# A transformer block on one core: query and key weights prepared in pairs, the values' first halves cast by VectorE, a new written order

## The chip, the cores and the metric

The kernel runs on one core of one Trainium2 chip. The metric is the device time of one execution in microseconds (us), median of several runs. Engine names as in the profile: PE is TensorE's matrix multiply, PEld its weight load, DVE is VectorE, ACT is ScalarE, POOL is GpSimd, SP is the engine whose queue issues the transfers.

## The reference

The input x has 8 sequences of 512 rows of 512 numbers. The block is attention, then a feed-forward part, each behind a layer norm and added to its input:

```
x = x + layernorm(attention(layernorm(x)))
x = x + layernorm(ffn(layernorm(x)))

attention: qkv = x @ w_attn + b_attn; 16 heads of 32; q and k are rotated by an angle
           that depends on head and column; causal softmax(q k^T) * 512**-0.5; times v; @ w_proj + b_proj
ffn:       y = quantised(layernorm(x)) @ ternary(w_fc).T ; gelu ;
           quantised(layernorm(.)) @ ternary(w_proj).T
ternary(w) = sign(round(w / (mean|w| + eps))) * mean|w|
```

All is float32. The kernel works with 16-bit matrix products and keeps the precision by splitting a number in two halves: `hi` is the number rounded to 16 bits, `lo` is what is left, rounded too.

## The kernel before, in words

**Work.** Attention goes by sequence b (8) and by group g of four heads (4 in a sequence); the feed-forward part goes by 128 rows (32 pieces). Each of these is a generator that records instructions and yields between steps. Every generator family has a letter: N normalises 128 rows of x, Q makes a group's queries and keys (12 + 12 matmuls of 512 columns, line 570), V makes 128 rows of values for 8 heads (12 matmuls of 256 columns, line 540), S makes a group's scores and their masked maxima (matmul 604, maxima on VectorE 618, 16 of them a group), A the exponentials and their halves (ScalarE 651 and 657, GpSimd 659, and a transposing transfer, 518), W the weighted sum of the values (686), G, P the projection, X, Z and C the feed-forward part (matmuls 817 and 873).

**Order.** The program order is written out as one string, `ORDER` (4345 letters): each letter takes the next step of that family, and `pin()` ties each instruction to the one before it on its engine. So every engine, and SP's queue of transfers too, does its instructions in the order in which the string recorded them. An instruction that waits holds all behind it on its engine. Tiles come from pools with a fixed number of buffers: PSUM has three `sc` tiles of two banks and two `mm` tiles of one bank.

**Start-up.** Before the first sequence can flow, weights are prepared (H, J, B, R, T, Y), which takes roughly the first 80 us, mixed with work of the first sequences:

- H and J call `make_qk_weights(s, g)` (227): s is 0 for queries and 1 for keys. The 128x512 block of the weight is transposed by a product with a unit matrix (235), copied to SBUF (240) and its rows' squares are summed (241); from the sums and the bias VectorE makes a bound per row and spreads it on a diagonal (244 to 247); one product with a matrix of ones brings all rows' bounds to every partition (254), VectorE takes the maximum (257), and from it makes a power of two as the scale (258 to 261). The transposed block is turned by the rotation angle (253), and is cut in two 16-bit halves (264 ScalarE, 266 VectorE). Then follow the scale of the scores and that of the bias (267 to 276). This is done 8 times. `rot`, an `sc` tile, is held from line 253 until line 266 has read it.
- R is `make_proj_weights`: row means of the projection's weight (350) are taken off (357, GpSimd), the largest magnitude is taken (367), its power of two gives the scale (373 to 379), and two halves are cut (383 to 386).
- `values` (V) ends in two reads of the same PSUM tile: ScalarE casts the first half (553), VectorE makes the second as a difference (555). The tile `mm` is free after both.

Of the kernel before, what the change touches and what calls it, by code (L numbers as in the profile page):

```python
# [10 lines left out]
F32 = mybir.dt.float32  # L11
F16 = mybir.dt.float16
BF16 = mybir.dt.bfloat16
I32 = mybir.dt.int32
# [21 lines left out]
nNwHwHHNNnwJHJwJNNNtNTNBNnHJBBBBBBBBNRNNHNJHRNRRBBNHNNHHHwJJRtTJJJHHNNBNnwHwBNJNRJJHwHRRNNNJHJJJ  # L36
RRttttttBHnwTNTNNJTNNNNNNQQHHTTTYJQQYYYHHNHHYtYHQYtYJQQQQIQHHJBYJYQQQHJTQQQSYYSQYQYSAQQttYYQQBtV
VSHSAQQAJAVYYNStVSAAAASYQQQAAAAAAJASQQQQAAQAAABBQQQVJQSASVVVSAAVnARVJVVAAJnVVVVnVSASAAAVVVARAVAV
VVSTTASQQQAVQQSQVVWWWVWnWAATWQVQVQQNNNAWWATWWSWNSWAWNNANNVAAAAAANWWVNVNVASNAAnQAANSAAAASWQSSTSAN
NASrAWNNWWAAGWAGASWWWWWWNAAWGVAAAAVAVAAVSVNNQSAAQQQWVVSQSVAAAAVAAQSAQVSGGGQQSAVAWSQWWWVWAAQQRRSA  # L40
AWWWWWWWAAAAAAQVWARVARAWQQQSSRAARQAAtSAAtQQQQQSSGAGAASQAWArWVWGWWAAWWVWWQWWWWWVASQQTTAGGSSYVGQAA
SAQAQAYAYYYYQSQYQQQYSPPAQPAYPPYAQAPSAWPSPAWVVVVFVAVVFAAAAAWAWWAPWYWPFFPPnPASSQQPWSVQFWnWAQAFWWAA
WSVSAQVAAFYQAAAAWAYQQSASVQQPNNSYPASQNFAAYAAAXQXXNNFAAANNXXNFXAXXPFXSPXFPGFPSrNWNVNWVNPSWWWAAWVGP
NSWAZAWWWWWAWAVAAVVAAVFSSVANVNYNAVAAYAYPVZSYVXZPPXXWZAAAAPXXXPGXPPXAFAGZFSXSrQWGQWnWZZXAWQWQVWSW
QWAZZQQWWQSSAAAZQWSQQWQZZCAAAAFZWWAAAAPCZAAAQSQSAAZCGQSCQQAAAAZSGQGCCWCZSVAAAWPGCVSVCCSVAASWWCWA
AAQAQWWCCQWQWSWWVWAAZQWAQNFVVFQVASWSQAAAVVQZAVFVSAWQGQGQQWAQASQZZCVQGVWWSPAAAWXWXXSAAQWnnQSQXAAA
VVQPSWWQFFNZWZPQPWPAAAWWAANZZZZrSZANAQAFXrQVPQVFXAWPQAXSVVQCQNXNCANPSPXCZWAnNWNNCASWWWNNWCQAAAFF
XSQPGZZCPGCAASWPWNSWPAnNFFSWCNZNAPVAAWWAASWXZVXXNPZNZNNPCCAAZFAZCVVVWAAAACAXASAVVVVZSZSZQSAVVXQX
QXFXFWPFVQXQQPAAWPXQPQFFSWNWNPAFFSWCCQAWPCZXAQZCXFPZCXrZZFAAAAAZQPFQFFPPCXZPZCZPGGGWWWWWWWAAASXC
PCFWSXCXPVXFSVAXAWAAZZASZCAAAZZZCCZCQAAVWVGCQZXAZZCCQZCSSCQCWWSCSWGAAQQWQCQSXZCGAGAQCWWXFXQPWWFA  # L50
AAAWWZZrAAAASCAWCACAAFCVQAAQCCWXXVXVVVGPNASGGZVZVSAAQXVQVZSQVPAFFQVXQSAFVQnPSXPNWWQAPQPnQWQWWFSA
AAAAZZZZPCZXWACZSCWWWWWCWZQQAVWAACZVAASXFSPPrWSXZXZZCSXAAVASSAVACQPGAAAACFASQASAAZCAACFXFXQXQXWZ
CCQGCXQQPXZFWrQWQWPWWPCZZZXPQFAFZXZZZPFNWCWZNXAACXWAQCWAAACWCNZAWCWZAPPNZZQCFXNNNPPSFFFFSFZnPCCN
ZNZAAXNnSCCPCZXXPZXXANNNNZXVPCACCrWNVZCZXCVVVZCVZASAANSAPSZCXASZCVAVAAAVCZAAZSSAAVVCVSQZPCCASAAA
AXCQCWWSQVCPQVXXWQQWXQWVFVNWQCrPAZQPZZZQPGGGXAPGFZZAQWSQXAQPSCWWAWQWWWACQASNXFACFZZFQCAAASWFCZWW
CAAZAQFQQCGGSXCFQWPWZZZXWWPSAAAAAGAQNFACXACAQAZWSFFFXCSACVWWVnWWWZAAQSQPFXXZZWVXXWAAGVVNXFXSQZAG
FXAQVVSQAGSSZQXXZQCCZVVQZAAAAZQFVQAXSQVVAWFCFFQAZCWZACQAQPCPZXSCSCWPCWPCASXWrAZWZAZZPZZXXZAAAAFA
CWCAAVAACCXCVSnAZSQPPVVrSPPSQCPWWWWWPQPAXAAAQSZZPCAZQFQZZFWCAAZZZSPPQCQCAAAWQFCQCQWCWNNCXWWXWSWG
PAAAAnXQVNGCAFCFFCWWWWWWWNCNNNWAAZVVFXVZAANZZCCNSVAPVSPAVSSVSFrNNAAAAFPAAACPSAAAAANXCNPAXFACXZZn
CXCXSSXZZNVNZFNCASXAPPCVVZACCAVFFCACCAAXXZZSXSXPFQCCPQrNWWFWAQWPXQXXWXPGGWSZZGQFZZQZZCWWZNXPAAAA  # L60
GWPWSAANAAZCZPWWWCAQSCQCQAZAZCQCZSQFAWGQAAZZACQSZQWCCCCQAAWSQQQVXZVSVVQWNWQWPAWQAPVGGQCWAVWWWWWW
XXAnAWSAQQASZSVVXZFGPFXXSQXQGZGCXQFAPAFFAASQASFPZZAAAAQQSAPAFAQAAPZXXQACSAQCSQQQZFFnCSCVWCWVAAZZ
APSWWWWVCFVVrWAWWVCPAZAZZWWAVVVWWAAASFAWnCZZACVCVVSXAAASPZCQFZZZCCXQACAASXAAAQXQQQQSQCSXQWCXCXQN
NXCXCANWCWWCWWZZFSNNNAAACANNAFAAXNNQNNNZQnFFZCVCGCGXWWWXWZWAWWWAFXCCVNFVVVSPNNVPXArZSSSZZAZAVPVS
QNAAAACSAAAAAPZAXXPQXXAQXPPZPPrQQPSQXSPAZQNPPZPZXSQXQFCQXCSAAPXCZZZZSWWCWCWWCAAAAAAFFAZAQAAZQVZC
AVXAZCVVPZAXPXWXPCZCSCFFFXPGGGWWZWPCXWCSWQWFQWFPCAGCAZAQSZSZAWACQZZAQQZCSSFAAACAAAZQNZWPGQCAFrQC
QCSWFQZQZACAVWVVGWWWCVWWWWWVWWCGACAZVAACSWGFVSSVFZVGXVXXVVVGSQXPAAAQPSAAZAVASXXQACrSVVPAQAFQPXFS
AFZAAQAZPXPFQWXZPZQZZNXCPSPPPAAQPQPWnWSWPZnWWQQCPZVCAAWZAAAASAFFFVVnZAVZSCZSCQCQWWQWQCWAWCAASAAA
SAAQQQAAWQCQXQZZNNZXNZCANZZWSXCCNAAACQNCNNCCXASSCWCQVCAZXNNNSCNSNWCWWXCWWCXXAFFAAZAAAGGWWWAWWFNA
rWNNWSCXAAAXVXWSCCCQXQQFVXZAAZAAQAVSVSSXAZPPFQQFAQSFZZZVAFAAAVXVQXPQXQXPZQQWWPXPZCSCArVPPZXZZZZV  # L70
XWWWVVVCVCXAZAXCWPPAZZAPVAVPXCPFZCPFZZZGFGGWSSCPWWWAZCSAAGAZAXPSQSWCQWWZAZZFAQFFFFXCQAXXAAACCWAF
AAACAASCZQCCXXQAZCXZQZACZSrCZQZCQASSWGWCAAWCWWZWACZGXWSCXSQXAAPPZCZCWWWWWWAAAACVAZCSrXZFGAXVQWQX
VXSXAZQCVCSFFFSQAGXPCQCAQCFSFCAZQZQZGZGASQCZAAAAAQCQAWSQQQCXZZFAZZZZAVCXCVVVXWPWAPWAAAAAFPAFWCCP
XPFPXWXVXCPWPFPFXZFZFSXASZCZrZZPVXZPZXPXXAVVACSXAPCSCQZZZZSACWWWWWQCAWAZACAQZFCSPFZPFFFPAFFAXXQW
CCQXQXAZZCCAZZCACWXXCrCZZZPACSWCSZPCPWCSPSCWWCAZZAZPAQAWSQXAZAZFASAAGGWAPPAAFQFXSAPQXCAFFSWWWZXZ
AZAQQPWAPSWWCFCCWPGAAAZAAAAXXPXXSXGAZGPAXAZCFSZZZAPCZSZZVVAFVVAAPAAZZAZACSCCSCGCCCCFAZArWSXZWWWW
WWWWWWWWXWXFSFAFASCASGAACCAPAFFAAAAAAZXAZXXCFXXXXZZZXXXXFCZFFFXZZZCCCGXCXWWCCXCWWWWWWWWWWWWZZGGC
GGZrZZZCXXCCXXZZCPXPZPCPCZPCZPPPCCZZrZFFXXCFFZZZZFXCFZFXCPCCZPCXCXCZZCCPXXZZCPPZPZCPZPFFFXFXPrXP
ZCPCCPPFPPZFZFZPXZZZCFZFXCXXCXXZZZFZCFPCXCCFFPFZCZXXXXZXCPXCCrXPPZZXPPPZZZZXFZZFXCZZFFZZFFFZCXCC
XCXCXXCZZZZCXXCCCCZCCZCZCXZXZZCCXCXXCXXCZZZZZZZZXZCXXCCZZCXZZXCZZZCZZCCCCCCCCCCZZCCCZZZZZCCZCCCC  # L80
CCCCCCCCCCCCCCCCCCCCCCCCC
# [4 lines left out]
def block_kernel(  # L86
# [40 lines left out]
    def sc_tile():  # L127
        return ps_sc.tile([P, 2, 512], F32, tag="sc", name="sc")
# [31 lines left out]
    def power_below(dst, src):  # L160

        nc.vector.tensor_scalar(
            dst.bitcast(I32), src.bitcast(I32), 0x7F800000, None, ALU.bitwise_and
        )

# [50 lines left out]
    qk_top = const.tile([P, 2 * NG], F32)  # L216
# [10 lines left out]
    def make_qk_weights(s, g):  # L227
        w = wraws.pop((s, g))

        n = s * NG + g
        pst = sc_tile()[:, 0, :]
        for k in range(NE):
            nc.tensor.matmul(pst[:, ts(k, P)], w[:, k, :], turns[:, NG, :], start=True, stop=True)
        yield
        wT = x1p.tile([P, E], F32, tag="x1", name="wT")
        sq = tp.tile([P, E], BF16, tag="q", name="sq", bufs=2)
        longest = tiny(2, f"long{s}")
        nc.scalar.copy(wT, pst)  # L240
        nc.scalar.activation(sq, pst, AF.Square, accum_out=longest[:, 0:1])
        yield
        b2 = longest[:, 1:2]
        nc.vector.tensor_tensor(b2, bqk[:, n : n + 1], bqk[:, n : n + 1], ALU.mult)
        nc.vector.tensor_scalar(b2, longest[:, 0:1], 2.0 * E, b2, ALU.mult, ALU.add)
        diag = tp.tile([P, P], BF16, tag="qT4", name="diag", bufs=2)
        nc.vector.tensor_scalar(diag, ident_h, b2, None, ALU.mult)
        yield

        ps = sc_tile()  # L250
        rot = ps[:, 0, :]
        for k in range(NE):
            nc.tensor.matmul(rot[:, ts(k, P)], wT[:, ts(k, P)], turns[:, g, :], start=True, stop=True)
        nc.tensor.matmul(ps[:, 1, 0:P], ones_b, diag, start=True, stop=True)
        yield
        top, sc = tiny(name=f"wtop{s}"), tiny(name=f"wsc{s}")
        nc.vector.tensor_reduce(top, ps[:, 1, 0:P], AX.X, ALU.max)
        nc.vector.tensor_scalar(top, top, 4.04, 2.0**-60, ALU.mult, ALU.max)
        root_power(top, top)
        nc.vector.reciprocal(sc, top)  # L260
        nc.vector.tensor_scalar(sc, sc, 2.0 ** (12 - 65) / X_S, None, ALU.mult)
        yield
        hi, lo = (wqk[s, g][:, h, :] for h in range(2))
        nc.scalar.activation(hi, rot, AF.Copy, scale=sc)
        yield
        nc.vector.scalar_tensor_tensor(lo, rot, sc, hi, ALU.mult, ALU.subtract)
        nc.vector.tensor_scalar(qk_top[:, n : n + 1], top, 2.0 ** (65 - 12), None, ALU.mult)
        nc.vector.tensor_scalar(
            bqk[:, n : n + 1], bqk[:, n : n + 1], sc, X_S, ALU.mult, ALU.mult
        )  # L270
        if s:
            nc.vector.tensor_tensor(
                e_scale[:, g : g + 1], qk_top[:, g : g + 1], qk_top[:, n : n + 1], ALU.mult
            )
            nc.vector.tensor_scalar(
                e_scale[:, g : g + 1], e_scale[:, g : g + 1], -1.0, None, ALU.mult
            )
        yield
# [756 lines left out]
```

## Time and profile before

| | |
|---|---|
| median of 3 runs | 1046.0 us (1045.74 to 1046.53) |
| profiled execution | 1048.4 us, its span 1046.6 us |
| PE busy | 974.4 us, 93% |
| ACT busy | 906.1 us, 87% |
| DVE busy | 824.9 us, 79% |
| POOL busy | 757.5 us, 72% |
| instructions | 22733 |

How to read it: an engine's busy time is the union of its instructions' spans. A group row gives line, engine, operation, the tile written and those read, shapes, then total busy time and the mean duration of one in ns, and behind the bar the engine's idle time just before these instructions and what ended it. A window row gives, for a stretch of time, busy us of each engine (instructions in brackets), the granted clock of TensorE as a fraction, and the transfers. The means of instructions that stand directly behind each other on an engine overlap a little at their ends: 512 maxima with a mean of 545 ns would be 279 us, but are busy for 253.4 us.

### The profile page before, as it was taken

What the parts mean: (1) busy time and instruction counts of PE and PEld (TensorE: products, weight loads), DVE (VectorE), ACT (ScalarE), POOL (GpSimd) and SP (SyncE); (2) the same over time, 40 slices, a digit from 0 to 9 for tenths busy, and PEclk for the clock granted to TensorE, in tenths of its full rate; (3) what the DMA queues carried; (4) which work ended last, traced back from release to release, by engine and by line L of the source; (5) the groups of instructions that cost most, each with busy time, mean ns of one, the idle gap of its engine ahead of it and who ended that gap; (6) DMA issues with size and microseconds to landing.
All of it is one profiled execution on the core that took longest, in us unless ns stands there. A gap on an engine that the chain in (4) does not pass through costs nothing.

```text
span 1046.6 us, 22733 instructions
## 1 busy us (share of the span) xinstructions
PE 974.4 (93%) x8258; PEld 509.0 (49%) x8258; DVE 824.9 (79%) x2482; ACT 906.1 (87%) x1504; POOL 757.5 (72%) x606
## 2 busy tenths in 40 slices
PE   6887889999899999999999999999999999999995
PEld 4444544545444544545545455454454454544442
DVE  6988779998788777887988787788777888866742
ACT  6879999999789998999899999899999889964552
POOL 4358868987677678787788688677867678865543
PEclk9989889999999999999999999999999999999997
DMA  8569999999899989999999999999999979995553
GB/s 265 180 140 185 197 214 159 192 181 207 167 175 178 206 166 164 172 170 188 182 194 178 162 193 177 165 165 189 182 171 173 166 145 173 198 200 117 101 101 80
DMA packets 585024, 181.07 MB, mean 173 GB/s; under 512 B 564304, under 2 KB 568400, under 8 KB 584912
## 3 DMA queue, kind: packets, MB, share of 16 engines
q1 hardware_dynamic: 584912, 179.63, 90.6%
q8 instruction: 64, 1.05, 0.4%
q14 instruction: 48, 0.39, 0.1%
HBM read 29.64 MB, written 8.39 MB: 36 GB/s over the span
## 4 chain that ended last, share of the span: by engine, by line
ACT 27%; PE 24%; DVE 13%; DMA 12%; POOL 12%; issue 9%; SPq 2%; POOLq 0%; ACTq 0%; DVEq 0%
PE sc L817 7%; ACT p L651 7%; POOL ph L659 6%; PE mm L873 5%; DMA pT<-ph 5%; ACT ph L657 4%; DMA qT<-q 4%; PE mm L570 3%; DVE p L618 3%; PE mm L731 3%; ACT junk L855 2%; ACT h L826 2%; PE sc L686 2%; ACT L826 2%; ACT q L768 2%
## 5 line engine op out<-in xcount | busy, mean ns | idle before, releaser
L659 POOL TENSOR_TENSOR ph<-p,ph 128x768 f16<-128x768 f32 (+1 forms) x192 | 355.1, 1852 | 109.0 <-ACT ph L657 96.8
L618 DVE CUSTOM_DVE_ANT_0 p<-sc,mask,e_scale 128x384 f32<-128x384 f32 (+3 forms) x512 | 253.4, 545 | 34.1 <-PE sc L604 17.9
L873 PE MATMUL mm<-wout,qT 128*128 128x512 fp8e4 x1024 | 259.5, 382 | 6.8 <-ACT row L891 5.0
L817 PE MATMUL sc<-wfc,qT 128*128 128x512 fp8e4 x1024 | 255.2, 379 | 5.8 <-DVE nmax L618 4.5
L651 ACT ACTIVATE p<-p,nmax 128x384 f32<-128x384 f32 (+3 forms) x512 | 253.0, 552 | 1.2 <-DVE nmax L618 0.7
L570 PE MATMUL mm<-xT,wqk 128*128 128x512 f16 x768 | 203.3, 383 | 2.4 <-DVE row L742 0.8
L657 ACT CAST ph<-p 128x768 f16<-128x768 f32 (+1 forms) x192 | 172.5, 899 | 4.7 <-DMA pT<-ph 1.7
L817 PEld LDWEIGHTS <-qT 128*128 128x128 f16 x1024 | 96.6, 98 | 118.8 <-issue 10.6
L873 PEld LDWEIGHTS <-qT 128*128 128x128 f16 x1024 | 94.7, 98 | 116.0 <-issue 14.8
L686 PEld LDWEIGHTS <-pT 128*128 128x128 f16 x2560 | 99.2, 98 | 60.6 <-DMA pT<-ph 18.2
L686 PE MATMUL sc<-vt,pT 128*128 128x65 f16 (+1 forms) x2560 | 103.7, 187 | 16.8 <-DMA pT<-ph 11.8
L540 PE MATMUL mm<-wv,xT 128*128 128x256 f16 x768 | 104.4, 277 | 6.9 <-DVE vt L555 2.8
L570 PEld LDWEIGHTS <-wqk 128*128 128x128 f16 x768 | 70.1, 98 | 81.5 <-issue 15.0
L731 PE MATMUL mm<-wp,oT 128*128 128x512 f16 x384 | 102.3, 379 | 1.3 <-DVE src L584 0.6
L851 POOL TENSOR_SCALAR h<-h,hnm,hqs 128x1024 f32<-128x1024 f32 x64 | 79.5, 1242 | 33.1 <-DVE hnm L847 31.4
L540 PEld LDWEIGHTS <-xT 128*128 128x128 f16 x768 | 73.4, 99 | 37.1 <-issue 11.2
L773 POOL TENSOR_TENSOR q<-h,q 128x1024 f16<-128x1024 f32 x32 | 68.7, 2147 | 24.6 <-ACT q L768 22.9
L604 PE MATMUL sc<-src 32*128 32x128 f16 (+3 forms) x1536 | 74.4, 300 | 11.0 <-DVE nmax L618 6.2
L855 ACT ACTIVATE junk<-h 128x1024 bf16<-128x1024 f32 x64 | 67.3, 1051 | 17.7 <-DMA qT<-q 14.0
L840 DVE TENSOR_REDUCE htop<-h 128x1 f32<-128x1024 f32 x64 | 76.4, 1211 | 6.1 <-ACT h L826 6.0
L768 ACT CAST q<-h 128x1024 f16<-128x1024 f32 x64 | 66.5, 1039 | 12.7 <-POOL h L851 11.2
L826 ACT ACTIVATE h<-sc,fsc 128x1024 f32<-128x1024 f32 x64 | 71.0, 1110 | 1.7 <-PE sc L817 1.1
(159 smaller groups left out, 1345.3 us busy)
## 6 DMA issues: line engine op xcount, KB each, us to landing
row<-in_x SPq DMA_DIRECT2D x32, 256.0 KB, 3.3
x<-in_x SPq DMA_DIRECT2D x32, 256.0 KB, 3.2
out<-row SPq DMA_DIRECT2D x32, 256.0 KB, 2.7
tw<-in_w_fcT SPq DMA_DIRECT2D x8, 512.0 KB, 7.7
tw<-in_w_outT SPq DMA_DIRECT2D x8, 512.0 KB, 4.8
wraw<-in_w_attn SPq DMA_DIRECT2D x8, 256.0 KB, 4.3
pT<-ph SPq DMA_TRANSPOSE x128, 5.6
qT<-q SPq DMA_TRANSPOSE x96, 4.3
```

Source lines behind the costliest of these rows:

```text
L540: nc.tensor.matmul(ps[:, :256], xT[:, c, hx, k, :], wv[hw][:, k, half * 256 : (half + 1) * 256], start=(n == 0), stop=(n == 3 * NE - 1),)
L570: nc.tensor.matmul(ps, w[:, hw, k, :], xT[:, :, hx, k, :], start=(n == 0), stop=(n == 3 * NE - 1),)
L618: nc.vector.tensor_tensor_reduce(p[:, j, at : at + (i + 1) * P], scs[t][:, j, at : at + (i + 1) * P], mask[:, T - (i + 1) * P :], e_scale[ ...
L651: nc.scalar.activation(pj, pj, AF.Exp, bias=nm[:, i, 2 * t + j : 2 * t + j + 1], scale=-1.0)
L657: nc.scalar.copy(hi, p)
L659: nc.gpsimd.tensor_tensor(lo, p, hi, ALU.subtract)
L686: nc.tensor.matmul(oo[:, j, i, :width], probs[u, PARTS[i]][:, half, j, STARTS[i] + c, :], vt[c][:, h, :width], start=(n == 0), stop=(n == ...
L731: nc.tensor.matmul(ps, oTs[b, k][:, ho, i, :], wp[hw][:, k, :], start=(n == 0), stop=(n == 3 * NE - 1),)
L817: nc.tensor.matmul(ps[:, o1, :], xsT[0][:, n // NE, n % NE, :], wfc[:, n % NE, ts(o, 512)], start=(n == 0), stop=(n == 2 * NE - 1),)
L826: nc.scalar.activation(h[:, ts(o2, 1024)], ps.rearrange("p a f -> p (a f)"), AF.Gelu, scale=xsc, accum_out=hsum[:, o2 : o2 + 1],)
L855: nc.scalar.activation(junk, hh, AF.Square, accum_out=hsq[:, o2 : o2 + 1])
L873: nc.tensor.matmul(ps, hT[0][:, half, k, :], wout[:, o2 * NF // 2 + k, :], start=(n == 0), stop=(n == 2 * NF - 1),)
```

## The change

**Pairs.** `make_qk_weights(g)` now does the queries' and the keys' block of a group in one generator (letter H; J is gone). The two sums of squares and the two biases stand in one 128x2 tile; the diagonal, the product that spreads it, and the maximum over 128 columns are replaced by one product of a matrix of ones with the 128x2 tile, whose result is already the sum over all rows (a sum in place of the largest). The steps on the small tiles that follow work on two columns at once, and the scores' scale is one instruction in place of two. Both `rot` halves now lie in one `sc` tile, and it is held until both second halves are made. The product for the bound goes to an `mm` tile.

**Projection.** The row means come from `bn_stats`, which gives the variance as well; the bound for the scale is made from the variance and `vinv`, so that the pass over 2048 columns for the largest magnitude (367) is gone. `root_power` takes the place of `power_below`.

**Values.** The cast of the first half is a VectorE instruction in place of a ScalarE one, 64 times.

**Order.** The string `ORDER` is new from the first letter to the last. It has the same number of steps of every family, with H at 57 in place of H at 29 and J at 28. The count of ScalarE's switches between its table of exponentials and that of the feed-forward part's function is 74 in both orders (counted in the recorded program).

```
-    def make_qk_weights(s, g):
-        w = wraws.pop((s, g))
-        n = s * NG + g
-        pst = sc_tile()[:, 0, :]
-        ...
-        nc.scalar.activation(sq, pst, AF.Square, accum_out=longest[:, 0:1])
-        yield
-        b2 = longest[:, 1:2]
-        nc.vector.tensor_tensor(b2, bqk[:, n : n + 1], bqk[:, n : n + 1], ALU.mult)
-        nc.vector.tensor_scalar(b2, longest[:, 0:1], 2.0 * E, b2, ALU.mult, ALU.add)
-        diag = tp.tile([P, P], BF16, tag="qT4", name="diag", bufs=2)
-        nc.vector.tensor_scalar(diag, ident_h, b2, None, ALU.mult)
-        yield
-        ps = sc_tile()
-        ...
-        nc.tensor.matmul(ps[:, 1, 0:P], ones_b, diag, start=True, stop=True)
-        yield
-        nc.vector.tensor_reduce(top, ps[:, 1, 0:P], AX.X, ALU.max)
-        nc.vector.tensor_scalar(top, top, 4.04, 2.0**-60, ALU.mult, ALU.max)
-        ...
+    def make_qk_weights(g):
+        longest, b2 = tiny(2, "long"), tiny(2, "b2")
+        sq2 = small.tile([P, 2], BF16, tag="sq2", name="sq2")
+        wTs = []
+        for s in range(2):
+            w = wraws.pop((s, g))
+            pst = sc_tile()[:, 0, :]
+            ...
+            nc.scalar.copy(wT, pst)
+            nc.scalar.activation(sq, pst, AF.Square, accum_out=longest[:, s : s + 1])
+            yield
+        bias = bqk.rearrange("p (s g) -> p s g", s=2)[:, :, g]
+        nc.vector.tensor_tensor(b2, bias, bias, ALU.mult)
+        nc.vector.scalar_tensor_tensor(sq2, longest, float(E), b2, ALU.mult, ALU.add)
+        yield
+        rot = sc_tile()
+        for s in range(2):
+            ...
+            yield
+        bound = mm_tile()[:, 0:2]
+        nc.tensor.matmul(bound, ones_b, sq2, start=True, stop=True)
+        yield
+        top, sc = tiny(2, "wtop"), tiny(2, "wsc")
+        nc.vector.tensor_scalar(top, bound, 2.04, 2.0**-60, ALU.mult, ALU.max)
+        root_power(top, top)
+        nc.vector.reciprocal(sc, top)
+        nc.vector.tensor_scalar(sc, sc, 2.0 ** (15 - 65) / X_S, None, ALU.mult)
+        yield
+        for s in range(2):
+            hi, lo = (wqk[s, g][:, h, :] for h in range(2))
+            nc.scalar.activation(hi, rot[:, s, :], AF.Copy, scale=sc[:, s : s + 1])
+            yield
+            nc.vector.scalar_tensor_tensor(
+                lo, rot[:, s, :], sc[:, s : s + 1], hi, ALU.mult, ALU.subtract
+            )
+            yield
+        nc.vector.tensor_scalar(top, top, 2.0 ** (65 - 15), None, ALU.mult)
+        nc.vector.scalar_tensor_tensor(bias, bias, X_S, sc, ALU.mult, ALU.mult)
+        nc.vector.scalar_tensor_tensor(
+            e_scale[:, g : g + 1], top[:, 0:1], -1.0, top[:, 1:2], ALU.mult, ALU.mult
+        )
+        yield
 ...
-        nc.vector.tensor_reduce(wm, raw, AX.X, ALU.add)
+        for k in range(NE):
+            nc.vector.bn_stats(st[:, k, :], raw[:, k, :])
+            nc.vector.bn_aggr(wst[:, k, :], st[:, k : k + 1, :])
 ...
-        nc.vector.tensor_reduce(
-            m, raw.rearrange("p k f -> p (k f)"), AX.X, ALU.max, apply_absolute_value=True
-        )
+        nc.vector.tensor_tensor(sq, wst[:, :, 1], vinv, ALU.mult)
+        nc.vector.tensor_tensor(sq, sq, vinv, ALU.mult)
+        nc.vector.tensor_reduce(m, sq, AX.X, ALU.max)
 ...
-        nc.scalar.activation(hi, v, AF.Copy, scale=back)
+        nc.vector.tensor_scalar(hi, v, back, None, ALU.mult)
 ...
-        "H": chain([qk_biases()], (make_qk_weights(0, g) for g in range(NG))),
-        "J": (make_qk_weights(1, g) for g in range(NG)),
+        "H": chain([qk_biases()], (make_qk_weights(g) for g in range(NG))),
```

## The prediction

> **What bounds the kernel now.** I read the page first: busy shares, then the rows of its 40 slices.
>
> ```profile
> PE 974.4 (93%) x8258; PEld 509.0 (49%) x8258; DVE 824.9 (79%) x2482; ACT 906.1 (87%) x1504; POOL 757.5 (72%) x606
> PE   6887889999899999999999999999999999999995
> DVE  6988779998788777887988787788777888866742
> ACT  6879999999789998999899999899999889964552
> PEclk9989889999999999999999999999999999999997
> ```
>
> The reader is to see that from the seventh slice (160 us) to the last but one PE is near 90% or above, and that PE's holes lie in the first six slices and the last. So I cut the span into stages with a windows query (columns as told above).
>
> ```profile
> 0.00:62.00 62.00, 42.78 (x279) 28.40 (x281) 52.39 (x180) 43.41 (x84) 25.66 (x40) 0.95 0.65 213
> 80.00:140.00 60.00, 47.12 (x601) 29.39 (x601) 46.77 (x157) 58.21 (x105) 52.99 (x39) 0.87 1.03 192
> 140.00:240.00 100.00, 91.26 (x953) 49.53 (x951) 93.09 (x291) 94.93 (x165) 81.61 (x58) 1.00 1.05 186
> 300.00:1000.00 700.00, 685.85 (x5654) 347.10 (x5654) 555.88 (x1620) 623.06 (x1011) 520.74 (x410) 1.00 0.93 171
> 1000.00:1046.60 46.60, 34.49 (x146) 14.66 (x144) 14.71 (x38) 18.17 (x28) 19.47 (x16) 0.88 0.40 89
> ```
>
> PE idles 19.2 us before 62, 12.9 from 80 to 140, 8.7 from 140 to 240, only 14.2 in the 700 us after 300, and 12.1 in the tail. A gain can come from these 72 us alone. Before 62 the fullest engine is VectorE (52.4 of 62, and idle mainly in the first 20 us), from 80 to 140 ScalarE (58.2 of 60), from 140 to 240 VectorE, ScalarE and PE together. Then the waits and PE's timeline:
>
> ```profile
> 60.10 0.61 PE L604 MATMUL sc<-src 32*128 32x512 f16 x2 [3.60 <-DVE wqk L266]
> 60.10:67.30 7.20, 6.55 (x31) 2.82 (x31) 7.01 (x22) 6.40 (x12) 4.16 (x3) 0.60 0.00 0
> ```
>
> The largest hole behind the first 10 us: scores need an `sc` tile that the weights' line 266 still holds, and just after it the granted clock is 0.60 over 7.2 us. The rows that price the parts:
>
> ```profile
> L555 DVE SCALAR_TENSOR_TENSOR vt<-mm,vt 128x256 f16<-128x256 f32 x64 | 26.7, 417 | 11.2 <-ACT vt L553 10.8
> L553 ACT ACTIVATE vt<-mm 128x256 f16<-128x256 f32 x64 | 24.4, 381 | 7.8 <-PE mm L540 5.0 <-PE sc L686 2.5
> L299 DVE TENSOR_SCALAR vs<-sc 128x512 f32<-128x512 f32 x1 | 0.7, 684 | 0.0
> L350 DVE TENSOR_REDUCE wmean<-wpraw 128x4 f32<-128x2048 f32 x1 | 2.3, 2275 | 0.0
> L367 DVE TENSOR_REDUCE pm<-wpraw 128x1 f32<-128x2048 f32 x1 | 2.3, 2275 | 0.0
> L257 DVE TENSOR_REDUCE wtop<-sc 128x1 f32<-128x128 f32 x8 | 2.3, 282 | 0.1
> L247 DVE TENSOR_SCALAR diag<-ident_h,long 128x128 bf16<-128x128 f16 x8 | 2.0, 254 | 0.4
> ```
>
> **The change part by part.** The sum is made on the profiled execution (span 1046.6, time 1048.4) and taken off the median, 1046.0, which lies 0.6 under that span.
>
> *Pairs.* VectorE before, per block: 182+214+254 ns (244 to 247), 282+154+154+164+154 (257 to 261), 743 (266), 143+203 (267, 268), that is 2.65 us; twice, with 0.33 for 272 and 275, 5.62 a group. After, by the same rows, two columns costing as one: 182+214, 154+154+164+154, twice 743, 143+203+173: 2.83 a group. Four groups save 11.2 us of VectorE, all early. ScalarE does what it did. PE loses eight 218 ns products and gains four of about 250 (line 438's shape): -0.7 us, where PE is idle anyway, so nothing. The bound now borrows an `mm` tile from Q and V until VectorE's line 258 has read it, four times; the nearest row is line 570's wait for line 451 (0.8 us, also a read of a product with ones): 0 to +3.2, I take 0, since PE idles in that stage.
>
> *Projection.* Removed 2.28+2.28 and 0.15; added 4x(0.686+0.182), two small products 0.36, a small reduction 0.15, `root_power` 0.15: -0.6 us of VectorE. ScalarE and GpSimd are not touched.
>
> *Casts.* ScalarE loses 64x0.381 = 24.4 us. VectorE's price: line 299 is a TENSOR_SCALAR out of PSUM, 512 columns in 684 ns; from 512 to 256 columns line 618 falls by 267 ns (746 to 479), so 417 ns, which line 555 of the same shape has too. Ends: 381 (ScalarE's) and 426. I take 0.42: +26.9 us (24.4 to 27.3). ScalarE's idle time before its cast (7.8 us, for PE) moves into VectorE's queue, and the 10.8 us that line 555 waited for ScalarE go: a wash. Behind a waiting cast on VectorE stand the next maxima, and behind those PE's scores, for their `sc` tiles. The page "VectorE: DVE Perf Modes" of the Trainium skill speaks against this part: under Specifications it places ScalarE closer to PSUM, and its errata section gives VectorE's PSUM reads 120 cycles plus one a column, at 0.96 GHz an estimate of 392 ns; by that the casts would be 25.1 us. The rows agree that VectorE is the slower one.
>
> *Along the order.* I counted each engine's work ahead of the last maximum, or exponential, of each head group in both recorded orders, each instruction at its mean; means overstate by a tenth (front part), so x0.9. VectorE, before and after: group 1 68.2 and 63.2, group 2 90.2 and 80.2, group 4 122.4 and 115.1, group 8 (about 220 us) 218.2 and 213.8, group 12 325.1 and 324.8, all 32 groups +14.6. ScalarE: group 2 84.0 and 81.0, group 4 120.0 and 118.0, group 8 219.8 and 212.6. GpSimd at group 8: 157.7 in both. So at group 8 VectorE is ahead by 4.0 us and ScalarE by 6.5; both are full between 140 and 240, the smaller saving rules: -4.0. Later VectorE's gain is paid back, but there it has 144 us idle of 700, and PE rules: nothing lost, and of ScalarE's 77 us idle a little more; I take -0.8 of PE's 14.2 (ends 0 and -4).
>
> *The hole at 57 us.* In the new order the last step of H stands at 187, the first scores at 201; before, the last J stood at 265, the first scores at 171. So no weight holds an `sc` tile when scores need one. The 3.6 us hole is part of VectorE's saving above; the clock behind it is not: 61.35 to 65.9 the chain runs on PE at half clock, 2.3 us lost. Saved if no other hole comes: 0 to -2.3, I take half, -1.2. "TensorE: Matmul & The Clock Gate", Part 1, says that the clock halves after an idle window of about 3.4 us; the 3.6 us fits, and by the rule alone the whole 2.3 would go.
>
> *Moved steps and queues.* On SP the values' weight now goes ahead of two query/key blocks, the projection's behind them; rows of x move. Rows that bound this: ScalarE waited 1.5 us for the values' weight, VectorE 3.4 for a row of x, PE 0.25 for the projection's weight: -3.4 to +3.4, I take 0, since about the same bytes come before the first turn. On GpSimd line 357 (3.0 us) goes from behind the first group's halves to ahead of them; covered by its 36 us idle before 62, else +3.0. ScalarE's queue now has a row's cast ahead of its first weight copy; it waited 5.5 us for PE there, which covers 0.6. The rest of the order: PE is 98% busy after 300, so a repacking moves little; 0, ends -4 and +4. The tail's last steps are much alike: 0, ends -3 and +3.
>
> Sum: -4.0 - 0.8 - 1.2 = -6.0, so 1040.0 us.
>
> **The rivals.**
> *Casts bind (slower).* Between 140 and 240 VectorE is busy 93.1 of 100 and gets 10 casts, +4.2. Its 6.9 us idle are waits for PE and GpSimd; if they stay, the stage grows by 4.2, and behind each late maximum stand scores on PE that wait for `sc` tiles. The early saving is lost if GpSimd, with equal work at group 8 and 53.0 busy of 60 from 80 to 140, sets the pace. Then 1050.2. It decides once more than 2.7 us of those 6.9 can't be filled. For: line 618 waits 15.2 us for GpSimd over the run. Against: ScalarE is fuller, at 94.9.
> *Hidden.* GpSimd's equal work alone holds the front, VectorE fits: 1046.0, give or take 2.
> *Front closes.* Both gate-backed holes (57 and near 91 to 101 us) go: ScalarE's 6.5, 2.3 of clock, 4 in the middle: 1033.2. For: 41 us idle of PE before 240. Against: GpSimd.
>
> **How the numbers follow.** Forecast (-10 to -2.1) 0.46, front closes 0.16, hidden 0.12, casts bind or a worse packing 0.26. Faster 0.62, within 0.2% (2.1 us, about what a measurement of this kernel can tell) 0.12, slower 0.26. The range reaches to both outer cases, 1033 to 1050, and leaves a part of each outside; the forecast's own range is 1036 to 1044.
>
> **What would show it.** Right: VectorE about 838 us busy, ScalarE 883, PE 973; no wait of 604 for the weights' second half; the clock full from 57 to 67; PE's idle time before 240 near 35 us in place of 41. Wrong: VectorE above 96 of 100 between 140 and 240 and PE waiting for maxima, or PE's idle time after 300 far from 14 us.

## The result: slower by 0.6%

| | before | after |
|---|---|---|
| median | 1046.87 us (1043.0 to 1052.74, 20 runs) | 1052.37 us (1046.26 to 1059.16, 20 runs) |
| ratio | 1 | 1.0057, 95% interval 1.0038 to 1.0076 |
| profiled execution, its span | 1048.4, 1046.6 us | 1049.1, 1047.3 us |

The forecast, 1040.0, had the sign wrong, and the time lies above its range (1033 to 1050). The profiled execution of the changed kernel is 3.3 us under its median, so one trace shows only part of the loss. Five more traces of it were taken (1054.28, 1046.97, 1051.54, 1049.34 and 1050.36 us), and where a mean over six is given below it is over these.

The page of the changed kernel, its busy shares and rows of 40 slices:

```profile
PE 973.2 (93%) x8254; PEld 507.2 (48%) x8254; DVE 832.9 (80%) x2503; ACT 891.8 (85%) x1440; POOL 756.9 (72%) x606
PE   6887888899999999999899999999999999999995
DVE  5887789998888878897788787898788888866742
ACT  6789989998799989999798998899899889964552
PEclk9997989999999999999999999999999999999998
```

TensorE's work is the same, VectorE has 8 us more and ScalarE 14 us less than before. The page alone doesn't say why the time grew. The same stages as before, by the windows view (us of the stretch, busy PE, PEld, DVE, ACT, POOL with counts, granted clock, DMA share, GB/s):

```profile
0.00:62.00 62.00, 44.49 (x300) 30.97 (x301) 45.47 (x148) 43.82 (x82) 24.95 (x41) 0.97 0.63 217
62.00:80.00 18.00, 16.07 (x137) 8.09 (x135) 16.05 (x52) 15.81 (x29) 14.77 (x10) 1.00 0.69 110
80.00:140.00 60.00, 47.45 (x618) 30.33 (x618) 47.55 (x165) 56.36 (x98) 52.72 (x37) 0.86 1.08 206
140.00:240.00 100.00, 91.01 (x929) 49.20 (x928) 94.90 (x297) 93.27 (x157) 76.58 (x56) 0.98 1.00 185
300.00:500.00 200.00, 195.12 (x1654) 99.95 (x1653) 164.20 (x487) 188.92 (x296) 150.43 (x116) 1.00 0.96 174
500.00:700.00 200.00, 193.04 (x1718) 100.28 (x1717) 164.53 (x499) 177.52 (x285) 155.38 (x124) 1.00 0.97 176
700.00:900.00 200.00, 197.77 (x1636) 98.53 (x1634) 165.49 (x487) 184.69 (x289) 149.88 (x114) 1.00 0.95 170
900.00:1000.00 100.00, 96.81 (x601) 45.39 (x600) 68.95 (x177) 62.09 (x102) 60.79 (x53) 1.00 0.75 146
```

VectorE before 62 us fell from 52.4 to 45.5, as the pairs were to do, and the clock from 62 to 80 is full: the 3.6 us hole of the scores at 57 us is gone, and in this trace the half clock behind it too. But TensorE's idle time before 240 us is 17.5 + 1.9 + 12.6 + 9.0 = 41.0 us, what it was before (37.6 to 41.7 in the six traces), and from 300 to 1000 us it is 17.3 us, 3.1 more than the 14.2 before (15.9 to 18.6 in the six). VectorE, which was to save, is fuller than before from 140 to 240 (94.9 against 93.1).

To see where the time goes along the order I took, for every trace, the moment at which the same amount of TensorE's work (matmul columns) was left, and subtracted that moment in the trace before. Negative is ahead, us:

```
moment in the trace before     112   218   239   301   499   521   657   937   1032
after, first trace            -2.5  +0.7  -0.7  -2.8  -3.4  -0.9  +1.3  +1.7  -0.5
after, mean of six traces     -2.3  +0.4  -1.1  -2.8  -3.4  -0.6  +2.0  +2.8  +0.8
after, fastest of the six     -2.8  -0.2  -1.8  -4.6  -5.3  -3.1  -2.3  -0.4  -2.5
after, slowest of the six     -1.3  +1.4  -0.2  -0.7  -0.8  +2.3  +5.2  +6.9  +4.8
```

So the front does gain, 2.3 us by 112 us, loses that by 218, and is 3.4 ahead at 499. Then 2.8 us go within 22 us, and more up to 657. At the very end of the program the mean of the six is 1.9 us behind. (The trace before is itself one of its longer executions, 1.5 us over the median of 20, so that is 3.4 over that median.)

### The profile page after: what moved, and what is told of

Same layout as the page of the kernel before. It is cut to its first block, busy times and chain, and to the rows that moved or that the text cites. A ratio compares the mean times of both kernels' runs of the same rounds, so it can differ in the third digit from the quotient of the medians.

```text
span 1047.3 us, 22667 instructions
## 1 busy us (share of the span) xinstructions
PE 973.2 (93%) x8254; PEld 507.2 (48%) x8254; DVE 832.9 (80%) x2503; ACT 891.8 (85%) x1440; POOL 756.9 (72%) x606
## 5 line engine op out<-in xcount | busy, mean ns | idle before, releaser
L664 POOL TENSOR_TENSOR ph<-p,ph 128x768 f16<-128x768 f32 (+1 forms) x192 | 353.6, 1846 | 91.8 <-ACT ph L662 79.6
L691 PE MATMUL sc<-vt,pT 128*128 128x65 f16 (+1 forms) x2560 | 104.8, 187 | 17.3 <-DMA pT<-ph 11.1
L545 PEld LDWEIGHTS <-xT 128*128 128x128 f16 x768 | 73.2, 99 | 38.3 <-issue 12.4
L773 ACT CAST q<-h 128x1024 f16<-128x1024 f32 x64 | 66.5, 1039 | 17.8 <-POOL h L856 14.9
```

The costliest lines, as they stand in the source:

```text
L545: nc.tensor.matmul(ps[:, :256], xT[:, c, hx, k, :], wv[hw][:, k, half * 256 : (half + 1) * 256], start=(n == 0), stop=(n == 3 * NE - 1),)
L664: nc.gpsimd.tensor_tensor(lo, p, hi, ALU.subtract)
L691: nc.tensor.matmul(oo[:, j, i, :width], probs[u, PARTS[i]][:, half, j, STARTS[i] + c, :], vt[c][:, h, :width], start=(n == 0), stop=(n == ...
```

## The experiments

### Which part costs: steps and orders crossed

Two edits to the order, two to the casts.

e1, the changed kernel's steps in the old order:
```
-nwwNnwHNNBwwntRNHHHHHNtNHwwtNnttHBtttBBBHw...
+nNwHwHHNNnwHHHwHNNNtNTNBNnHHBBBBBBBBNRNNHN...   (the old string, each J read as H)
```


> The changed steps (pairs, projection, casts on VectorE) recorded in the old order: every J of the old string is read as an H, so that the joint generator takes the old places. Three theories. ORDER: the loss of the change (1052.4 against 1046.9) comes from the new string, whose holes in PE's work in the stretch where PE is the bound let the granted clock drop in some executions; then these steps in the old order are as fast as before or a little faster, 1042 to 1047. CASTS: the 64 casts on VectorE cost the time, wherever they stand: 1050 to 1054. PAIRS: the joint generator, which holds an sc tile longer, costs the time: 1050 to 1054, and more here than in the new order, since scores are interleaved with it.

e2, the old kernel's steps in the new order (the new string's 57 H are read as 29 H and 28 J):

> The steps of before recorded in the new order: the new string's H are read as H or J in turn (the query's and the key's step at the places of the joint generator's steps). ORDER: as slow as the changed kernel or slower, 1052 to 1056, with times spread over more than 8 us. CASTS: as before, 1045 to 1048. PAIRS: as before, 1045 to 1048.

e3, the kernel before, with one line changed:
```
-        nc.scalar.activation(hi, v, AF.Copy, scale=back)
+        nc.vector.tensor_scalar(hi, v, back, None, ALU.mult)
```


> Before with one line changed: the values' first half is cast by VectorE. ORDER: within 2 us of before, 1045 to 1049, VectorE busy about 849. CASTS: 1051 to 1054. PAIRS: as before, 1045 to 1048.

e4, the changed kernel with that line put back:

> The changed kernel with one line undone: ScalarE casts the values' first half again. ORDER: still 1050 to 1056, and still spread. CASTS: back to 1045 to 1048. PAIRS: as the changed kernel, 1051 to 1054.

Later, with the same question, e5: the changed kernel's pairs and projection in the old order, with ScalarE's cast:

> The queries' and keys' weights made in pairs and the projection's bound from variances, in the old order of steps (each J read as H), casts of the values on ScalarE as before. The 11.2 us that VectorE saves early are there. SAVING (they shorten the front whatever the order): 1041 to 1045. FIT (the old order was laid out for the separate weights; the pair's later steps come before their inputs are there, as its sister kernel with VectorE's casts showed, 8 to 10 us behind at 110 us): 1047 to 1056. That sister took 1070.0, and the casts alone in the old order 1068.2, so a plain difference gives 1048.8.

Measured, with the kernel before beside each on the same chip:

| | order | casts on | median us | ratio to before, 95% |
|---|---|---|---|---|
| e1 | old | VectorE | 1070.03 | 1.0213 (1.0194 to 1.0231) |
| e2 | new | ScalarE, no pairs | 1114.00 | 1.0631 (1.0611 to 1.0652) |
| e3 | old, no pairs | VectorE | 1068.23 | 1.0185 (1.0162 to 1.0208) |
| e4 | new | ScalarE | 1104.93 | 1.0558 (1.0529 to 1.0588) |
| e5 | old | ScalarE | 1059.74 | 1.0110 (1.0082 to 1.0138) |

None of the simple theories stands: neither the order, nor the casts, nor the pairs is "the" loss. Each order fits its own steps. The casts alone cost 1.9% in the old order, the pairs and the projection alone 1.1%, and taking the casts back in the new order costs 52.6 us, nearly ten times the loss itself. 64 instructions of 0.4 us are worth 21 us when moved to VectorE in the old order and 53 us when moved back in the new one, so their price is not their duration. What it is in the old order can be read in e3, whose program differs from before in that line alone. The waits on the values' two halves (553, 555) and on the maxima (618) before:

```profile
PE mm L540 <- DVE vt L555: 2.8, 5, 0.8
PEld L540 <- DVE vt L555: 1.1, 1, 1.1
PE mm L731 <- DVE vt L555: 0.4, 1, 0.4
DVE vt L555 <- ACT vt L553: 10.8, 12, 2.0
ACT vt L553 <- PE mm L540: 5.0, 7, 1.7
PE sc L604 <- DVE nmax L618: 6.2, 6, 2.0
PE sc L817 <- DVE nmax L618: 4.5, 4, 2.4
```

and in e3 (waiter, what it waited for, us in all, times, longest):

```profile
PEld L540 <- DVE vt L555: 8.2, 12, 2.0
PE mm L540 <- DVE vt L555: 6.0, 10, 1.5
PEld L570 <- DVE vt L555: 3.6, 7, 1.0
PE mm L731 <- DVE vt L555: 2.3, 3, 1.2
PEld L731 <- DVE vt L555: 2.0, 5, 0.7
PE mm L570 <- DVE vt L555: 1.0, 2, 0.5
DVE vt L553 <- PE mm L540: 10.3, 8, 3.0
PE sc L817 <- DVE nmax L618: 9.8, 7, 2.7
PE sc L604 <- DVE nmax L618: 9.2, 10, 2.0
```

VectorE's wait for ScalarE (10.8) is gone and a wait for TensorE (10.3) stands in its place: that is the exchange the prediction had called a wash, and between these two it is one. But a VectorE that stands 10.3 us at the head of its queue, or comes late to the second half, holds two kinds of tiles. One is the `mm` tile that it reads, which TensorE borrows for queries, values and projection: with 0.3 us for line 438 in both, TensorE's matmuls stood 3.5 us for line 555 before and stand 9.6 in e3, 6.1 more. (The PEld rows are waits of the weight loads; they overlap with these waits and with running matmuls, so they aren't added.) The other is the `sc` tiles that late maxima hold, which TensorE needs for scores (604), weighted sums and the feed-forward part (817): with 1.7 and 2.2 us for line 686 these waits were 12.4 us before and are 21.2 in e3, 8.8 more. Together that is 14.9, in an execution 14.0 us longer than the profiled one of before (by the medians 21.3); other waits went up and down, the longest, line 686's for transposed halves, from 11.8 to 6.5. In the changed kernel, by the same view, the two are 3.7 and 4.8, together less than before: the new order has room for VectorE's casts. In e4 the other side shows: VectorE's second half now follows a cast that is queued on ScalarE without room for it:

```profile
DVE vt L560 <- ACT vt L558: 44.3, 30, 5.4
ACT vt L558 <- PE mm L545: 40.1, 22, 3.8
PE mm L545 <- DVE vt L560: 10.7, 5, 4.1
PE mm L575 <- DVE vt L560: 9.0, 6, 3.0
POOL ph L664 <- ACT ph L662: 111.4, 75, 5.6
```

GpSimd waits 111.4 us for ScalarE's halves where the changed kernel has 79.6.

e5 shows where the pairs pay: it is 12.6 us behind at 112 us of the trace before and 11.9 at 1032, so its whole loss is made in the front. From 62 to 80 us its TensorE does 12.2 us of work against the changed kernel's 16.1. Between 20 and 90 us it stands 4.5 us before the values' bias (1.4 before), 3.6 before scores for maxima and 2.0 before the product of the pairs' bound: many small lags of steps that come in the old slots before their inputs are there, none of which is the whole.

### Which half of the order loses

The two strings have taken exactly the same steps at letter 2126 (about 470 us), so halves can be joined, the casts going with their half:
```
+        if at[0] < 2126:
+            nc.vector.tensor_scalar(hi, v, back, None, ALU.mult)
+        else:
+            nc.scalar.activation(hi, v, AF.Copy, scale=back)
...
-    for k in "".join(ORDER.split()):
+    for at[0], k in enumerate("".join(ORDER.split())):
```


> The first 2126 letters of the new string (to about 470 us), with the changed steps and the casts on VectorE, then the old string from there with the casts on ScalarE. At letter 2126 both strings have taken the same number of steps of every family. In the profiles PE's work stands 3 us ahead of before at 470 us in the changed kernel, and level at the end. SECOND HALF: what the changed kernel loses, it loses behind 470 us, by the packing of its second half; then 1042 to 1045, with a spread as of before. FRONT: it loses by holes in the first 240 us that let the clock drop in some executions; then 1048 to 1056 and a spread of 8 us or more.

> The mirror: steps and string of before for the first 2126 letters, casts on ScalarE, then the new string with the casts on VectorE. SECOND HALF: 1050 to 1055, with the changed kernel's spread. FRONT: 1045 to 1049.

h1 (new first half, as in the lines above) took 1049.98 us, ratio 1.0037 (1.0015 to 1.0059); h2 (old first half, new second) 1050.69, ratio 1.0039 (1.0018 to 1.0060). So either half, put in alone, costs about the same, and the loss can't be given to one of them. In its trace (1047.19, one of its shorter executions) h1 is 4.8 us ahead at 499 us, with pairs, new front and VectorE's casts, and has 0.4 left at 1032, over a second half that is the old one letter for letter. Here a lead carried into a stage wasn't a gain at its end.

Beside them two more traces of the changed kernel were taken, to see how far executions differ:

> The changed kernel once more, for a second execution to lay beside the first (its runs lie from 1046 to 1059). If it lands above 1055: SECOND HALF says that PE's work is as far ahead at 470 us as in the first profile and that the time goes behind it, with a half clock somewhere between 470 and 1000 us; FRONT says that it is behind by 240 us.

> The changed kernel a third time, as the run before it: a third sample of where the time goes in a slow and in a quick execution.

They took 1054.28 and 1046.97 us, the ends of the table of progress above. The lead at 499 us is 0.8 in one and 5.3 in the other, at the same program. Yet the larger holes in TensorE's work behind 240 us stand at the same steps in all six traces of the changed kernel: 1.4 to 2.2 us at 273, 1.6 to 2.3 at 350, 1.4 at 496 and 2.0 to 2.2 at 516.

### Are the holes the loss?

These holes can be seen in the timeline of the changed kernel (start, us, instruction, times; in brackets idle time and what ended it):

```profile
272.16 0.81 PE L736 MATMUL mm<-wp,oT 128*128 128x512 f16 x3
275.05 0.39 PE L691 MATMUL sc<-vt,pT 128*128 128x65 f16 x8 [2.09 <-DMA pT<-ph]
...
349.47 0.81 PE L575 MATMUL mm<-xT,wqk 128*128 128x512 f16 x3
351.94 0.82 PE L736 MATMUL mm<-wp,oT 128*128 128x512 f16 x3 [1.65 <-DMA oT<-hT]
...
515.15 1.02 PE L822 MATMUL sc<-wfc,qT 128*128 128x512 fp8e4 x4
518.41 0.95 PE L691 MATMUL sc<-vt,pT 128*128 128x65 f16 x28 [2.24 <-DMA pT<-ph]
519.21 0.82 PE L545 MATMUL mm<-wv,xT 128*128 128x256 f16 x6
519.87 1.03 PE L822 MATMUL sc<-wfc,qT 128*128 128x512 fp8e4 x4
```

At 516 us TensorE stands before a product with weights whose transposed halves are still in transfer, while the products that stand next in the order (545, 822) are ready. The kernel before has 3 holes over 0.85 us between 300 and 900 us (0.9, 1.7 and 0.9); the changed one has 1.65, 0.9, 1.4, 2.2, 1.1 and 1.1 there. x1 moves, at four such places, only steps that are TensorE's alone behind ready ones, so that no other engine's order changes:

```
-WCWCW   -PSXAWW   -WWWPAAWWQ   -WWWWZFNNVNXCC
+CCWWW   +SXAWWP   +PAAQWWWWW   +ZFNNVNXCCWWWW
```


> The changed kernel with four holes of TensorE behind 270 us filled in its order: at each, steps that only TensorE works on (products of W, P) change places with the neighbours that were ready, so no other engine's order changes. The holes are 2.1, 1.7, 1.4 and 2.2 us in the changed kernel's trace, 7.3 together. PACKING theory (the changed order loses its early lead in a few places where the step that stands next on TensorE isn't ready): 1045 to 1049, 3 to 7 us under the changed kernel's 1052, and TensorE's idle time after 240 us falls by about 5. Rival LATE RESULTS (the holes are where the other engines or the transfers are behind anyway, so the wait moves to the next step that needs them): 1051 to 1053, idle time the same, at other lines. Half-clock spells behind the holes go in the first case, so a little of the gain may be theirs.

x1 took 1046.70 us, ratio 0.9994 (0.9968 to 1.0020): the whole loss is gone. By progress it gains 2.2 us on the mean of the changed kernel's six traces from 258 to 301 us, 1.3 from 342 to 401, and 2.5 from 499 to 521, that is 6.0 at three of the four places; in its one trace it is 5.7 ahead of that mean at 1032 us and 4.0 at the end. Its idle time from 240 us on was to fall by about 5; it is 31.0 us, against 31.2 to 34.5 in the six (mean 33.1), so 2.1 less. Another part goes with the clock, which behind 240 us is at half for 5.7 us in x1's trace and for 8.2 to 12.8 in the six. At 508 us another hole of 1.3 us takes the place of that at 496. Its timeline at the place of the largest, where 545 and 822 now stand ahead of 691:

```profile
512.74 0.82 PE L545 MATMUL mm<-wv,xT 128*128 128x256 f16 x6
513.39 1.03 PE L822 MATMUL sc<-wfc,qT 128*128 128x512 fp8e4 x4
514.25 0.94 PE L691 MATMUL sc<-vt,pT 128*128 128x65 f16 x28
515.05 0.81 PE L545 MATMUL mm<-wv,xT 128*128 128x256 f16 x6
```

The same treatment of the kernel before, and of the hybrid h1:

> The kernel before with the same treatment of its three largest holes behind 270 us (1.7 us at 577 and two of 0.9): steps of W and X that only TensorE works on stand behind ready neighbours, the three X at the third hole behind V too. PACKING: 1043.5 to 1045.5, that is 1 to 3 us faster than before. LATE RESULTS: 1046 to 1047.5. A loss of over 3 us would say that any touch of a tuned order costs, however small.

> The changed order and VectorE's casts up to 470 us, the old order and ScalarE's casts behind it (that hybrid took 1050.0, with 1045.4 as the span of its profiled execution), with two holes of the first half (2.1 at 273 and 1.7 at 350 us) and one of the second (1.7 us) filled as in the two kernels of this batch. PACKING: 1042 to 1047, faster than before by up to 0.4%. LATE RESULTS: 1049 to 1051.

x2 took 1049.41, ratio 1.0009 (0.9992 to 1.0027), no gain: the holes of 1.5 and 2.4 us at 267 and 280 came back as 1.5 and 2.8 at 278 and 283, since what stood first then wasn't ready either, and only the hole at 577 shrank (1.7 to 1.2). In these kernels such a move gained where the next step was ready, and not elsewhere. x3 took 1044.79, ratio 0.9981 (0.9953 to 1.0009), against 1.0037 for the same order with its holes.

One hole in the stage from 140 to 240 us is of another kind. The timeline of VectorE in the changed kernel, while TensorE stands 2.07 us before the values' product (545), at 184.6:

```profile
183.88 0.69 DVE L156 BATCH_NORM_STATS2 st<-row 128x6 f32<-128x512 f32 x1 [0.77 <-DMA row<-in_x]
184.62 0.18 DVE L157 BATCH_NORM_AGGREGATE mvn<-st 128x2 f32<-128x6 f32 x1
184.83 0.15 DVE L500 TENSOR_SCALAR nr<-mvn 128x1 f32<-128x1 f32 x1
184.90 0.14 DVE L501 TENSOR_SCALAR nn<-mvn 128x1 f32<-128x1 f32 x1
184.96 1.36 DVE L780 SCALAR_TENSOR_TENSOR q<-row,fqs,q 128x512 f16<-128x512 f32 x1
186.25 0.41 DVE L560 SCALAR_TENSOR_TENSOR vt<-mm,vt 128x256 f16<-128x256 f32 x1
```

The values' second half (560) stands behind a row that is still in transfer and a 1.36 us operation; TensorE goes on just behind it. x4 is x3 with two such second halves moved up to stand right behind their first (`VYSFSQ...FPPFV` to `VVYSFSQ...FPPF`):

> The hybrid with its holes filled (changed order to 470 us, old order behind it), and two more steps of VectorE moved: for the values of the turns near 158 and 174 us the second part (hi and lo are both made on VectorE there) stands directly behind the first; it stood 8 and 12 us later, behind rows' statistics and a 1.7 us feed-forward operation, and TensorE waited 2.07 us at 184 for the tile that it reads. LATE LOW PART theory: with the cast on VectorE these waits are part of what the casts cost; the hole at 184 goes, TensorE's idle time from 140 to 240 falls by 1.5 to 2.5 us, the time by 1 to 2.5. Rival VECTORE FULL (95.9 busy of 100 in that stage): the hole moves to the next product that needs VectorE, idle time and time the same within 1.

x4 took 1043.89 us, ratio 0.9971 (0.9948 to 0.9993): it is faster than the kernel before, by 0.3%. But TensorE's idle time from 140 to 240 fell by 0.4 us only (91.88 us busy against 91.48 in x3), not by 1.5 to 2.5: the hole at 184 shrank to 0.9 and now waits for maxima, that at 151 (1.7) is gone, one at 165 grew from 1.1 to 1.7, and the rest is spread. In that stage VectorE is busy 95.6 of 100, and the rival, VECTORE FULL, holds. The gain over x3 (0.9 us by the medians) is within the intervals.

### The half clock

Three more traces of the changed kernel were taken for its longest executions:

> The changed kernel again, for one more trace. Six of its 20 timed executions took 1057.8 to 1059.2 and had 53 to 61 us at half clock by their mean clock, the other fourteen 29 to 50 us and 1046.3 to 1055.5; of 40 to 50 executions of the kernel before none was over 1054.5. EARLY SPELL theory: in the long ones the half clock lasts longer in the new front (the 13.7 us spell that starts at 93 us, or the one at 33), since kernels with the old front and the new second half had at most 42 us. SPREAD theory: many single spells of 3.4 us behind holes all along the order.

> The same kernel as the run before it, for a second trace; the two theories as there.

> The same kernel again, for a third trace; the two theories as there.

They took 1051.54, 1049.34 and 1050.36 us; none is one of the longest, so where those spend their half clock stays open. Of the early spells, one of 10.2 us at 33 us stands in a1, a3 and a5 and in none of the other three; those with it took 1050.4 to 1054.3 us and stand 1.1 us worse at 112 us, those without it 1047.0 to 1049.3. Three against three is a hint, no proof. The traces together show what goes ahead of a spell. The spells (stretches at half clock), in us from the start and their lengths, for the same hole at 516 us and that at 273:

```
                 hole at 273   half clock behind it   hole at 516   half clock behind it
first trace      2.09          none                   2.24          none
a1               2.07          3.4 at 275.8           2.05          3.4 at 521.5
a2               1.42          none                   2.06          none
a3               2.16          3.4 at 275.8           2.07          3.4 at 521.5
a4               1.81          none                   2.05          3.4 at 517.3
a5               1.94          none                   2.20          3.4 at 518.2
```

From 258 to 278 us a1 and a3 lose 4.7 and 4.8 us against the trace before, the other four 2.4 to 3.1: a spell there costs nearly 2 us. So a hole of 2 us has a half clock behind it in some executions and none in others. In every trace the spells begin on a grid of 3.413 us that runs through the whole execution, whatever the work. I therefore divided 18 traces (all above, with that of the kernel before) into these 3.413 us windows, from 12 us to three windows before the end, and counted by TensorE's busy share in a window whether the clock of the next was half:

```
clock in the window   busy share      windows   next one at half clock
full                  under 0.45         99       97
full                  0.45 to 0.60      139       44
full                  0.60 to 0.65       61        1
full                  over 0.65        4920        0
half                  under 0.70         35       35
half                  0.70 to 0.85       24       19
half                  0.85 to 0.95       35        3
half                  over 0.95         104        6
```

A 2 us hole is 0.6 of a window if it falls inside one, and two parts, each harmless, if a border halves it; the grid's place against the work differs from execution to execution. Between 140 and 1000 us, the number of windows under 0.55 busy, averaged over all places of the grid, is 2.0 in the trace before, 3.6 to 4.7 in the changed kernel's six, 4.1 in h1, 2.4 in x1, 2.3 in x3 and 1.5 in x4 (but also 2.1 in h2, which is slower than before, so the count is not all). So holes are paid twice: by themselves, and by the chance of a half-clock window behind them. Over the first 22 timed executions of the changed kernel and 34 of the one before, the time at half clock (twice the span times one less the mean clock) has a median of 42.9 us in the changed kernel and 39.7 before, and the span is longer by 0.3 us for each us of it; that is about 1 of the 5.5 us. The page "TensorE: Matmul & The Clock Gate" of the Trainium skill, Part 1, gives a free-running window of 3413 ns, with which the grid agrees, and has the clock fall after an idle window of about 3.4 us. Here no idle window was needed: over 1.9 us idle in a window (under 0.45 busy) sufficed in 97 of 99, and 1.4 to 1.9 us (0.45 to 0.60) in 44 of 139. The measurement decides.

## Why the prediction was wrong

**Pairs, -11.2 us of VectorE: right in kind, too large.** The rows that the prediction lists for a group after the change add up to 3.03 us, not 2.83, so its own working gives 10.4. The rows of these steps sum to 22.5 us before and 13.7 in the changed kernel, 8.8 less; one of the four instructions of line 271 took 1.97 us where the others took 0.16, for a reason that the trace doesn't show. Busy time before 62 us fell by 6.9 us and TensorE was 2.3 us ahead at 112. Put into the old order, the pairs and the projection cost 1.1% (e5).

**Casts, VectorE's price: right; ScalarE's gain: too large; "a wash": wrong in the old order.** The cast took 0.42 us as estimated:

```profile
L558 DVE TENSOR_SCALAR vt<-mm x64: 412/420/433, 45.5 to 907.2; 128x256 f16<-128x256 f32 x64
```

(minimum, median, maximum ns). ScalarE's busy time fell by 14.3 us, and by 12.6 in e3, where only the 64 casts left and every other row kept its duration, not by 24.4: neighbours on an engine overlap (10.5 of the casts' 24.4 us in the trace before lie under other instructions of ScalarE), so a short instruction's row is more than what its removal frees. Nor were the waits a wash: exchanged in place (e3), they made TensorE wait 8.8 us more for maxima, the path that the prediction had named and left without a price, and 6.1 us more for the `mm` tiles that the casts read, which it had not looked for. In the changed kernel the two waits are 4.8 and 3.7 us, against 12.4 and 3.5 before, so they are not what it lost by.

**Along the order, -4.0 at group 8: wrong.** At 218 us the mean of six is 0.4 behind, at 239 it is 1.1 ahead. VectorE was 4 us ahead by count, but its last maximum of group 8 ended at 211.6 us in the first trace against 213.0 before, 1.4 ahead. It gave only a part of its saving on: it was fuller from 140 to 240 (94.9 of 100), as the rival *casts bind* had it, and its second halves came late for TensorE there (the 2.07 us at 184). That rival's mechanism, late maxima with scores behind them, is the larger part of what e3 shows; that it is the place of the loss in the changed kernel is not shown, since moving two second halves up freed 0.4 us.

**The hole at 57 us, -1.2: about right at its place, paid back at others.** From 57 to 67 us the clock is full in the first trace; in the other five one window of 3.4 us at half clock is left there, where before there were two:

```profile
57.00:67.00 10.00, 9.16 (x76) 4.25 (x76) 8.97 (x34) 9.20 (x19) 8.46 (x9) 1.00 0.00 1
57.00:67.00 10.00, 9.51 (x81) 4.27 (x81) 8.97 (x34) 9.29 (x19) 8.04 (x9) 0.83 0.00 1
```

(first trace, and a1). That mostly one window of two went is about what the prediction's half came to, by luck: it had taken the middle between the whole and nothing. In the six traces the total at half clock is 33.9 to 52.4 us, against 40.7 in the trace before.

**"A repacking moves little; 0, ends -4 and +4", with the -0.8 for later: the step that decided the sign.** TensorE went from 3.4 us ahead at 499 to 0.8 behind at 1032, 4.2 us that the sum had at nothing, with 1.1 more in the tail, which was at nothing too. In that stretch and ahead of it stand holes of 1.4 to 2.2 us at steps that stood before ready ones; x1 moves steps at four of them, gains at two before 499 us and at one behind it, and has the whole loss back. That PE was 98% busy behind 300 us I took for a sign that nothing could change there. It says that 14 us of idle time were all there was to win, and nothing of how much there was to lose. The prediction's own sign of being wrong, idle time after 300 far from 14 us, is 17.3 up to 1000 us in the first trace and 15.9 to 18.6 in the six.

**Moved steps, 0.** TensorE's wait at the start is 5.6 us, for the first weight, in place of 5.4 for constants, and GpSimd waits 17.9 us in a row for a row's statistics. TensorE is 3.6 us behind at 55 us in the first trace, and 4.0 ahead at 70, once the kernel before has paid for its hole at 57. Covered by then, as assumed.

What stays open: the longest executions (6 of 20 over 1057 us), of which no trace was caught. The median of the other fourteen is 1049.98, 3.1 us over the kernel before, about what the six traces show (3.4); the rest of the median's 5.5 comes with the long ones. They aren't explained by the four holes: x1 still has 2 of 12 at 1055 us and x3 has 3 of 12 at 1053 to 1055, all with 51 to 59 us at half clock by their mean clock.

## What to carry to other kernels

When an order is written out by hand or by a planner, an instruction moved to another engine is priced by whom it makes wait: ask who needs the tile that it reads and what stands behind it in its new queue, and lay out the order anew, or not at all. A stage that is 98% busy can't gain much, but a new order can lose in it; look in the new trace for holes where the next step in the order is ready and the present one isn't, and change those two on the bound engine alone. Compare medians of many executions, not single traces, when holes are near 2 us, since here the clock made of the same hole at 273 us now 2 us and now 4.

## What the runs showed of the hardware that was not expected

In these 18 traces the clock of TensorE followed its busy share in fixed windows of 3.413 us: below 0.45 the next window was at half clock (97 of 99), over 0.65 never (0 of 4920), and from half clock it mostly came back with a window over 0.85 (9 of 139 stayed). The grid's place against the work differed from execution to execution. The same program took 1046.3 to 1059.2 us, and its executions with more half clock were the longer ones, by 0.3 us for each us; that the grid's place makes the whole of this spread isn't shown.
